# Latent attention block: block 3's scores as two lanes of 64 rows, and Pool's row moves dealt out behind heads

## The chip, the cores and the metric

The kernel runs on one core of one Trainium2 chip. The core has a matrix engine (TensorE, PE in the profile; its weight loads are shown apart as PEld), a vector engine (DVE), a scalar engine (ACT), a general engine (Pool), a queue engine that issues most transfers (SP), and 16 DMA engines. Matmul results go to PSUM, a memory of eight banks of 512 float32 columns on 128 partitions; all other tiles lie in SBUF. The metric is the device time of one execution in microseconds.

## The reference, cut to what matters

One layer: multi-head latent attention over 2048 tokens with a causal mask, a residual and a layer norm, then a linear layer with another residual and norm. 16 heads have 128 content dimensions and 64 rotary dimensions; the rotary part of the key is shared by all heads.

```python
cq = rms_norm(hidden_states @ w_qa.T, q_a_ln_w)                 # 2048 x 384
q = (cq @ w_qb.T).reshape(b, s, H, DQ).transpose(0, 2, 1, 3)    # H = 16, DQ = 128 + 64
q_nope, q_pe = q[..., :DN], q[..., DN:]
q_pe = q_pe * cos + rotate_half(q_pe) * sin
ckv = hidden_states @ w_kva.T                                   # 2048 x (128 + 64)
k_pe = ckv[..., KVLR:]; k_pe = k_pe * cos + rotate_half(k_pe) * sin
ckv_l = rms_norm(ckv[..., :KVLR], kv_a_ln_w)
kv = (ckv_l @ w_kvb.T).reshape(b, s, H, DN + DV).transpose(0, 2, 1, 3)
scores = (q_nope . k_nope + q_pe . k_pe) * scale                # per head, causal
attn = softmax(scores); out = attn . v
x = layernorm(x + out @ w_o.T)
x = layernorm(x + x @ (weight * scale_weight).T + bias)
```

## The kernel before, in words

The key projection is folded into the queries, so that all heads share one key of 128 latent rows. Precision is kept by splitting every operand into a high and a low float16 part: `Kn[:, 0]` and `Kn[:, 1]` are the high and low parts of the latent keys (128 rows, 2048 columns), `qn` the same for the queries. For the rotary part, a tile `pe` holds the high part of a head's 64 rotary query rows in partitions 0 to 63 and the low part in 64 to 127; `Kp[:, 0]` holds the rotary keys' high part in both halves of the partitions, `Kp[:, 1]` their low part. A score chunk is thus five matmuls of 128 rows (`score`, L682): qn high by Kn high, qn high by Kn low, qn low by Kn high, and pe by Kp high and by Kp low. The last of them also multiplies low by low.

The work goes by four query blocks of 512 rows (`b`), in each by eight pairs of heads (`p`), in a pair by four query tiles of 128 rows (`qt`), and for blocks 1 to 3 by the two heads `j` of the pair (`units`, L983). Block 3 comes last and has the longest rows: a query tile sees 1664, 1792, 1920 or 2048 keys for qt 0 to 3. `chunks` (L44) cuts them into four: two of 512, and two of 320, 384, 448 or 512. The first two chunks make the head's first score tile, the last two its second; a tile takes two PSUM banks. Block 3 has three such tiles in rotation ("s", "s", "u" by `state["turn"]`, L728); the other two banks are the tiles "m" of values and projections.

For each head `head_scores` (L714) issues, in this order: the score matmuls of the first tile, its maximum on DVE (L740), the next steps of the head before (`next(prev)`), the score matmuls of the second tile, its maximum, then the bias (L750), two exponentials on ACT with their sums (L756), and the inverse of the sum (L768, L769). `head_probs` is that generator `prev`: ACT writes the high half of the scaled probabilities (L777, two cuts), DVE the low half (L780, two cuts), and SP transposes them into `ring` (L784). In block 3 the first cut of L780 stands between the two maxima for qt 2 and 3 and behind them for qt 0 and 1 (L744). The causal mask lies in the last tile's last 128 columns: as a matmul of `identb` by `maskb` (L697) for j = 0, as an addition on DVE (L701) for j = 1, right behind the tile's matmuls.

Between heads PE has other work, in program order: half of the value products of an earlier query tile (`values`, L822; the lag is two query tiles in block 3), and the projections for the next pair, spread by `at` (L990 to L1005): `project_nope` behind heads 3 and 4 of a pair, `project_pe` behind heads 0 and 1 of every second pair. `project_pe` (L607) makes the rotary rows of four heads at once: PE and DVE make the products (L564, L569), Pool combines them (L631, L632), copies eight groups of 32 high rows into `pe` (L635) and, after ACT has rounded them (L638), writes eight groups of low rows (L640). A group serves two pairs, and it is made while the pair two ahead of its first use runs.

From query tile 1 of block 3's first pair on, the order on PE, SP, DVE and ACT is the order of the code (`manual_schedule`, L1009); Pool's is left to the scheduler. Before that a scheduler orders DVE, ACT and Pool.

Of the kernel before, what the change touches and what calls it, by code (L numbers as in the profile page):

```python
# [19 lines left out]
P = 128  # L20
# [6 lines left out]
QB = 512  # L27
NPAIR = H // 2
# [8 lines left out]
W_O = 32768.0  # L37
X_UP = 1024.0
PROBS = 10240
TINY = 1.0e-30  # L40
NEG = -1.0e30

# [16 lines left out]
def mla_block(ctx: ExitStack, tc: tile.TileContext, a, out):  # L59
    nc = tc.nc  # L60
    ET = mybir.EngineType
# [32 lines left out]
    identb = const.tile([P, P], BF16, name="identb")  # L94
    nc.vector.tensor_copy(identb, ident)
    maskb = const.tile([P, P], BF16, name="maskb")
# [28 lines left out]
    Kn = kv.tile([P, 2, S], F16, name="Kn")  # L125
    Kp = kv.tile([P, 2, S], F16, name="Kp")
# [14 lines left out]
    psum = {}  # L141
# [366 lines left out]
    state = {"queue": nc.sync}  # L508
    later = []
# [74 lines left out]
    def rope_stack(pe, ph, cols, js, eng=nc.vector):  # L584

        for j in js:
            q = slice(32 * j, 32 * j + 32)
            for x in range(2):
                yield eng.tensor_copy(pe[32 * x : 32 * x + 32, j, cols], ph[q, 0, x, cols])
                yield eng.tensor_copy(pe[64 + 32 * x : 96 + 32 * x, j, cols], ph[q, 1, x, cols])  # L590

    stack, soon = [], []

    def run_soon():
        while soon:
            soon.pop(0)()
# [10 lines left out]
    def project_pe(b, g):  # L607

        if ("wpe", b, g) not in state:
            load_wpe(b, g)  # L610
        w = state.pop(("wpe", b, g))
        cq, cs = state["cq"], state["cs"]
        every = slice(0, QB)
        prod = prj.tile([P, 2, 2, QB], F32, tag="prod", name=f"prod{b}_{g}")
        for x in range(2):
            ps = psum["m"].tile([P, QB], F32, tag="m", name=f"ps_pe{b}_{g}_{x}")
            rope_products(w, cq, cs, prod, ps, x, every)
            if x == 0:
                yield
            elif b or g == 3:  # L620
                load_wpe(*((b, g + 1) if g < 3 else (b + 1, 0)))
        ph = prj.tile([P, 2, 2, QB], F16, tag="ph", name=f"ph{b}_{g}")
        pe = blk.tile([P, 8 if (b, g) == (0, 3) else 4, QB], F16, tag="pe", name=f"pe{b}_{g}")
        if b == 0 or (b, g) == (1, 0):
            rope_split(b, prod, ph, every, (nc.gpsimd, nc.gpsimd), nc.vector)
            stack.append(rope_stack(pe, ph, every, range(2 if b else 4)))
            for _ in rope_stack(pe, ph, every, range(2, 4 if b else 2), nc.gpsimd):
                pass
        else:
            rp, tp = prod[:, 0], prod[:, 1]  # L630
            nc.gpsimd.tensor_tensor(rp[:, 0, :], rp[:, 0, :], rp[:, 1, :], ALU.subtract)  # L631
            nc.gpsimd.tensor_tensor(rp[:, 1, :], tp[:, 0, :], tp[:, 1, :], ALU.add)  # L632
            rows = [(j, x, slice(32 * j, 32 * j + 32)) for j in range(4) for x in range(2)]
            for j, x, q in rows:
                nc.gpsimd.tensor_copy(pe[32 * x : 32 * x + 32, j, :], rp[q, x, :])  # L635

            def low_rows():
                nc.scalar.activation(ph[:, 0], rp, AF.Copy)  # L638
                for j, x, q in rows:
                    nc.gpsimd.tensor_tensor(  # L640
                        pe[64 + 32 * x : 96 + 32 * x, j, :], rp[q, x, :], ph[q, 0, x, :], ALU.subtract
                    )

            soon.append(low_rows)
        state["pe", b, g] = pe
        yield
# [56 lines left out]

    def take(n):

        at = state.get("probs_at", 0)
        if at + n > PROBS:
            at = 0  # L710
        state["probs_at"] = at + n
        return probs_mem[:, at : at + n]

    def head_scores(pools, b, p, j, qt, nk, prev):  # L714
        r = er[1][:, p // 2 : p // 2 + 1]
        cks = chunks(nk)
        nt = len(cks)
        neg = small.tile([P, 2], F32, tag="neg", name="neg")
        tiles = []
        for ti, ck in enumerate(cks):  # L720

            if b == 2 and ti == 1:
                ps = psum["t"].tile([P, 1, 512], F32, tag="t", name=f"s{b}_{p}_{qt}_{j}_{ti}", bufs=2)
            else:
                k = "s"
                if b == 3:

                    state["turn"] = (state.get("turn", -1) + 1) % 3  # L728
                    k = "ssu"[state["turn"]]
                ps = psum[k].tile(  # L730
                    [P, 2, 512], F32, tag=k, name=f"s{b}_{p}_{qt}_{j}_{ti}", bufs=3 if b == 1 else 1 if k == "u" else 2
                )
            w = ck[0][1]
            for ci, (c0, w) in enumerate(ck):
                d = nk - P - c0
                score(ps[:, ci, :], c0, w, b, p, j, qt, d if 0 <= d < w else None)
            v = ps[:, : len(ck), :w]
            if ti == nt - 1 == 0:
                next(prev, None)
            nc.vector.tensor_reduce(neg[:, ti : ti + 1], v, axis=AX.XY, op=ALU.max, negate=True)  # L740
            tiles.append((v, ck[0][0], len(ck), w))
            if ti < nt - 1:
                next(prev, None)
                if b < NB - 1 or qt > 1 and (p, qt, j) != (NPAIR - 1, 3, 1):  # L744
                    next(prev, None)
        bias = small.tile([P, 1], F32, tag="bias", name="bias")
        if nt == 1:
            nc.vector.tensor_scalar(bias, neg[:, 0:1], r, None, ALU.mult)
        else:
            nc.vector.tensor_scalar(bias, neg[:, 0:1], neg[:, 1:2], r, ALU.min, ALU.mult)  # L750
        for _ in prev:
            pass
        pr = take(nk)
        sums = small.tile([P, 2], F32, tag="sums", name="sums")
        for ti, (v, c0, n, w) in enumerate(tiles):
            nc.scalar.activation(  # L756
                pr[:, c0 : c0 + n * w].rearrange("p (a c) -> p a c", a=n),
                v,
                AF.Exp,
                bias=bias,  # L760
                scale=r,
                accum_out=sums[:, ti : ti + 1],
            )
        inv = small.tile([P, 1], F32, tag="inv", name="inv")
        if nt == 1:
            nc.vector.tensor_scalar(inv, sums[:, 0:1], 1.0 / P_UP, None, ALU.mult)
        else:
            nc.vector.tensor_scalar(inv, sums[:, 0:1], sums[:, 1:2], 1.0 / P_UP, ALU.add, ALU.mult)  # L768
        nc.vector.reciprocal(inv, inv)  # L769
        return pr, inv  # L770
# [114 lines left out]
    with tc.manual_schedule(engines={ET.PE}):  # L885
        x = [split_x(0, [x_r[0][:, kt : kt + 2] for kt in (0, 2)], nc.gpsimd)]
# [36 lines left out]
        ph = prj.tile([P, 2, 2, QB], F16, tag="ph", name="ph0_0")  # L923
        pe = state["pe", 0, 0] = blk.tile([P, 4, QB], F16, tag="pe", name="pe0_0")
# [58 lines left out]
    def units(pool, ring, b, norms=None):  # L983
        lag = min(ring.shape[1] // (2048 * (b + 1)) - 1, 3) if b else 4

        for p in range(NPAIR):
# [7 lines left out]
            else:  # L994
                at = (3, 4)
# [10 lines left out]
            for qt in range(4):  # L1006
                nk = (4 * b + qt + 1) * P
                if (b, p, qt) == (NB - 1, 0, 1):
                    ctx_f.enter_context(tc.manual_schedule(engines={ET.PE, ET.SP, ET.DVE, ET.Activation}))  # L1009
                if (b, p) == (0, NPAIR - 1) and qt >= 2:  # L1010
                    spare = state["qn", 0, p][:, 2:] if qt == 2 else state["pe", 0, 3][:, 4:]
                    s0 = -4 * nk
# [7 lines left out]
                if nk <= 512:  # L1020
                    pi = pair_scores(pool, b, p, qt, nk)
                    probs.append(pair_probs(pool, b, p, qt, nk, PT, *pi))
                    flush()
                    for step in plan[p][qt]:
                        if step == "F":
                            fill()
                        else:
                            next(side[step == "W"], None)
                    move_rows(6)
                    run_values(lag)  # L1030
                    run_values(lag)
                else:
                    for j in range(2):
                        prepare_output(b, p, 2 * qt + j)
                        prev = probs.pop() if probs else iter(())
                        pi = head_scores(pool, b, p, j, qt, nk, prev)
                        probs.append(head_probs(pool, b, p, j, qt, nk, PT, *pi))
                        if (b, p, qt, j) == (1, 0, 1, 0):
                            half_values()
                            half_values()  # L1040
                        run_soon()
                        if 2 * qt + j in at:
                            fill()
                        if b == 2 and (2 * qt + j) % 4 == 2:
                            next(norms, None)
                        run_values(lag)
# [103 lines left out]
    while len(vals) > 2:  # L1150
# [5 lines left out]
    ring = ctx_m.enter_context(tc.tile_pool(name="rings", bufs=1, reuse_waits="tile")).tile(  # L1156
        [P, 12 * 2048], F16, name="ring"
    )
    probs_mem = ctx_m.enter_context(tc.tile_pool(name="probs", bufs=1, reuse_waits="tile")).tile(
        [P, PROBS], F32, name="probs"  # L1160
    )
# [253 lines left out]
```

## Time and profile before

| | us |
|---|---|
| median of the runs (three: 1507.42, 1507.46, 1510.05) | 1507.46 |
| the profiled execution | 1508.39 |
| its span | 1506.6 |
| PE busy | 1455.3 |
| DVE busy | 1168.2 |
| ACT busy | 937.7 |
| POOL busy | 355.2 |
| block 3's scores, first to last (812.57 to 1262) | 449.4 |

Times in the profile are microseconds from the span's start unless marked ns. A row of the timeline is start, duration, engine, line, operation, output<-input with shapes, how many, and in brackets how long the engine was idle before it and what released it. A row of a window is its bounds and length, then the busy time of PE, PEld, DVE, ACT and POOL with the number of instructions, the granted clock of PE as a share of full speed, the share of the DMA engines and GB/s. Matmuls overlap: a row's duration includes the way through the array, and the step from one start to the next is what a matmul costs in a stream.

### The profile page before, as it was taken

Reading aid. Unit: us, or ns where it says so; the run is one execution under the profiler, and the core shown is the slowest. Engines: PE = TensorE matmul, PEld = TensorE weight load, DVE = VectorE, ACT = ScalarE, POOL = GpSimd, SP = SyncE. Lnnn points to the kernel's source line nnn. Section 1 sums busy time; section 2 is a strip of 40 time slices with the busy share of each in tenths; the row PEclk is TensorE's granted clock in tenths of the full one; section 3 lists DMA queues with packets and bytes.
Section 4 is the critical chain, followed back from the end, with each engine's and each line's share of the span. In section 5 each row is a group of like instructions: output and inputs, shape, how many; then the busy total and the mean of one; then the engine's idle time right before and its main releaser. Section 6 shows DMA issues by size and latency. Waiting matters only on the chain.

```text
span 1506.6 us, 24573 instructions
## 1 busy us (share of the span) xinstructions
PE 1455.3 (97%) x9056; PEld 907.1 (60%) x9056; DVE 1168.2 (78%) x2173; ACT 937.7 (62%) x1695; POOL 355.2 (24%) x412
## 2 busy tenths in 40 slices
PE   8899988999999999999999999999999999999997
PEld 6667754666665566666666666666666665544444
DVE  4787787988888988888888877877877786476654
ACT  6577775666675787778776666666666675432300
POOL 4223313451305405050023500500500000032132
PEclk9899999999999999999999999999999999999999
DMA  5569775878887998989896787787787898655431
GB/s 202 145 162 218 176 183 112 159 146 171 160 186 154 177 189 175 196 179 175 163 199 137 152 163 154 149 163 154 138 159 156 187 217 172 244 155 146 147 92 42
DMA packets 642377, 246.90 MB, mean 164 GB/s; under 512 B 598864, under 2 KB 619600, under 8 KB 641616
## 3 DMA queue, kind: packets, MB, share of 16 engines
q1 hardware_dynamic: 640800, 243.46, 75.1%
q8 instruction: 71, 1.16, 0.3%
q10 hardware_dynamic: 1152, 1.31, 0.3%
q0 software_dynamic: 304, 0.56, 0.1%
q14 instruction: 50, 0.41, 0.1%
HBM read 67.57 MB, written 28.05 MB: 63 GB/s over the span
## 4 chain that ended last, share of the span: by engine, by line
PE 63%; DVE 3%; DMA 1%; issue 1%; ACT 1%; POOL 0%; POOLq 0%; DVEq 0%; ACTq 0%; SPq 0%
PE s L695 27%; PE o L833 17%; PE acc L1134 9%; PE ps_qn L653 4%; PE ff L1283 3%; PE ps_pe L564 2%; PE ps_wo L297 1%; DVE probs L780 1%; DMA ring<-probs 1%; DVE neg L740 1%; ACT probs L756 0%; DMA xt<-xs 0%; DVE bn L1244 0%; ACT probs L777 0%; DVE x L1256 0%
## 5 line engine op out<-in xcount | busy, mean ns | idle before, releaser
L695 PE MATMUL s<-Kn,qn 128*128 128x512 f16 (+5 forms) x1920 | 462.9, 347 | 9.7 <-DVE qn L73 4.9
L756 ACT ACTIVATE probs<-s,bias,er 128x1024 f32<-128x1024 f32 (+3 forms) x320 | 324.1, 1016 | 204.4 <-issue 68.4
L780 DVE SCALAR_TENSOR_TENSOR probs<-probs,inv 128x1024 f16<-128x1024 f32 (+7 forms) x320 | 355.0, 1130 | 28.3 <-ACT probs L777 26.4
L833 PEld LDWEIGHTS <-V 128*128 128x128 f16 x3264 | 319.1, 98 | 87.2 <-issue 15.1
L833 PE MATMUL o<-ring,V 128*128 128x256 f16 x3024 | 361.0, 273 | 2.0 <-DMA ring<-probs 1.3
L740 DVE TENSOR_REDUCE neg<-s 128x1 f32<-128x1024 f32 (+3 forms) x320 | 316.9, 993 | 38.2 <-PE s L695 34.7
L695 PE MATMUL s<-Kp,pe 128*128 128x512 f16 (+5 forms) x1280 | 340.1, 347 | 0.9 <-DVE pe L590 0.9
L777 ACT ACTIVATE probs<-probs,inv 128x1024 f16<-128x1024 f32 (+7 forms) x320 | 294.2, 959 | 72.7 <-DVE inv L769 50.0
L695 PEld LDWEIGHTS <-qn 128*128 128x128 f16 x1920 | 187.6, 98 | 154.3 <-issue 13.7
L695 PEld LDWEIGHTS <-pe 128*128 128x128 f16 x1280 | 124.6, 98 | 107.3 <-DVE pe L590 1.6
L653 PE MATMUL ps_qn<-cq,wq 128*128 128x512 f16 (+1 forms) x594 | 139.2, 382 | 7.6 <-ACT ot L838 3.6
L640 POOL TENSOR_TENSOR pe<-prod,ph 32x512 f16<-32x512 f32 x88 | 123.8, 1407 | 5.7
L1134 PE MATMUL acc<-wvo,oh 128*128 128x512 f16 (+1 forms) x424 | 124.1, 375 | 0.9 <-ACT probs L756 0.9
L631 POOL TENSOR_TENSOR prod<-prod 128x512 f32<-128x512 f32 x11 | 14.0, 1271 | 443.8 <-DVE prod L569 443.8
L653 PEld LDWEIGHTS <-wq 128*128 128x128 f16 x594 | 59.4, 101 | 70.5 <-issue 12.7
L1134 PE MATMUL acc<-wvo,ol 128*128 128x512 f16 (+1 forms) x212 | 79.5, 375 | 0.0
L768 DVE TENSOR_SCALAR inv<-sums 128x1 f32<-128x1 f32 x128 | 26.9, 210 | 66.0 <-ACT probs L756 65.4
L72 ACT ACTIVATE oh<-o,kvo 128x1024 f16<-128x1024 f32 x26 | 29.8, 1146 | 71.0 <-PE acc L1134 58.0
L1134 PEld LDWEIGHTS <-oh 128*128 128x128 f16 x424 | 41.5, 98 | 50.8 <-issue 5.2
L635 POOL CAST pe<-prod 32x512 f16<-32x512 f32 x88 | 66.6, 757 | 14.0 <-PE o L833 10.6
L564 PE MATMUL ps_pe<-cq,wpe 128*128 128x512 f16 (+1 forms) x306 | 68.2, 367 | 1.7 <-DVE wpe L73 0.9
L838 ACT ACTIVATE ot<-o 128x256 f32<-128x256 f32 x128 | 48.3, 378 | 28.7 <-PE o L833 27.6
(214 smaller groups left out, 1553.9 us busy)
## 6 DMA issues: line engine op xcount, KB each, us to landing
ot_d<-ot SPq DMA_DIRECT2D x128, 128.0 KB, 2.6
o<-ot_d SPq DMA_DIRECT2D x32, 512.0 KB, 4.0
wq<-wq_d SPq DMA_DIRECT2D x30, 384.0 KB, 3.8
wpe<-wpe_d SPq DMA_DIRECT2D x15, 384.0 KB, 3.7
nw<-in_wo_dram SPq DMA_DIRECT2D x8, 512.0 KB, 4.2
wo<-in_wo_dram SPq DMA_DIRECT2D x4, 1024.0 KB, 5.6
x<-in_x_dram SPq DMA_DIRECT2D x16, 256.0 KB, 3.5
out_dram<-xb SPq DMA_DIRECT2D x15, 256.0 KB, 2.0
```

Source lines behind the costliest of these rows:

```text
L564: nc.tensor.matmul(ps, w[:, i, lt, x * P : (x + 1) * P], cq[:, tiles(cols), k, lt], start=n == 0, stop=n == 3 * LT - 1)
L635: nc.gpsimd.tensor_copy(pe[32 * x : 32 * x + 32, j, :], rp[q, x, :])
L640: nc.gpsimd.tensor_tensor(pe[64 + 32 * x : 96 + 32 * x, j, :], rp[q, x, :], ph[q, 0, x, :], ALU.subtract)
L653: nc.tensor.matmul(ps, w[:, i, lt, j * P : (j + 1) * P], cq[:, tiles(cols), k, lt], start=n == 0, stop=n == 3 * LT - 1)
L695: nc.tensor.matmul(ps[:, :w], lhs, K[:, i, c0 : c0 + w], start=n == 0, stop=n == 4)
L740: nc.vector.tensor_reduce(neg[:, ti : ti + 1], v, axis=AX.XY, op=ALU.max, negate=True)
L756: nc.scalar.activation(pr[:, c0 : c0 + n * w].rearrange("p (a c) -> p a c", a=n), v, AF.Exp, bias=bias, scale=r, accum_out=sums[:, ti : ti ...
L777: nc.scalar.activation(hl[:, 0, c], pr[:, c], AF.Copy, scale=inv)
L780: nc.vector.scalar_tensor_tensor(hl[:, 1, c], pr[:, c], inv, hl[:, 0, c], ALU.mult, ALU.subtract)
L833: nc.tensor.matmul(ps[:, :256], vt[:, k % 4, i, :], v[:, :, l, k, :], start=n == 0, stop=n == 3 * kts - 1)
L838: nc.scalar.activation(ot, ps[:, :256], AF.Copy)
L1134: nc.tensor.matmul(acc[:, cols], l[:, t, c], state["wvo"][p][:, i, j, cols], start=p == 0 and j == 0 and n == 0, stop=p == NPAIR - 1 and j ...
```

## The change

In block 3 (`b >= ROWS`) a head's scores are made by a new function, `scores_by_rows`. A matmul of 128 rows becomes two of 64: the lower one on partitions 0 to 63, the upper one on 64 to 127, each on a part of the array of its own. The two lanes work at the same time on two key chunks, which lie in two PSUM banks. There are four rounds: (0,1), (2,3), (1,0), (3,2), the first number being the chunk of the lower lane. In a round each lane runs high by Kn high, high by Kn low, low by Kn high, and its half of pe by Kp high. The product of the rotary high rows by Kp low is made once, in the first two rounds; for the upper lane the high rows are needed on partitions 64 to 127, and a new tile `again` holds that copy, written by a DMA on SP, once a pair (`rope_again`). The product of low by low is left out. A chunk so takes nine halves, and a head 36 matmuls and 36 weight loads in 18 steps where it had 20.

Between rounds one and three, and two and four, a lane meets a bank that the other lane has written. An empty Pool instruction (`keepalive_nop`) waits for the earlier round, and the later round waits for it.

Both score tiles of a head are taken before its first matmul, and all its score matmuls are issued before its first maximum. The mask matmul of j = 0 comes last; the mask addition of j = 1 is issued on DVE ahead of both maxima.

Pool's order is the code's too from the same point on. For the rotary groups 1 to 3 of block 3, the eight high-row copies and eight low-row subtractions are no longer issued at once but dealt out behind the following heads, three copies or two subtractions behind each (`by_pool`).

```diff
+ROWS = 3
...
+    by_pool = []
...
-            for j, x, q in rows:
+
+            def high_row(j, x, q):
                 nc.gpsimd.tensor_copy(pe[32 * x : 32 * x + 32, j, :], rp[q, x, :])
+
+            def low_row(j, x, q):
+                nc.gpsimd.tensor_tensor(
+                    pe[64 + 32 * x : 96 + 32 * x, j, :], rp[q, x, :], ph[q, 0, x, :], ALU.subtract
+                )
+
+            later = b >= ROWS and g > 0
+            for r in rows:
+                if later:
+                    by_pool.append((3, lambda r=r: high_row(*r)))
+                else:
+                    high_row(*r)
+            if later:
+                by_pool.extend((2, lambda r=r: low_row(*r)) for r in rows)
 
             def low_rows():
                 nc.scalar.activation(ph[:, 0], rp, AF.Copy)
-                for j, x, q in rows:
-                    nc.gpsimd.tensor_tensor(
-                        pe[64 + 32 * x : 96 + 32 * x, j, :], rp[q, x, :], ph[q, 0, x, :], ALU.subtract
-                    )
+                if not later:
+                    for r in rows:
+                        low_row(*r)
...
+    def rope_again(b, p):
+
+        again = state["again", b, p] = psum["again"].tile([P, 2, QB], F16, tag="again", name=f"again{b}_{p}")
+        nc.sync.dma_start(again[64:], state["pe", b, p // 2][:64, 2 * (p % 2) : 2 * (p % 2) + 2])
+
+    def scores_by_rows(parts, b, p, j, qt, masked):
+
+        qs = slice(qt * P, (qt + 1) * P)
+        qn = state["qn", b, p]
+        high, low = qn[:, 0, j, qs], qn[:, 1, j, qs]
+        rope, again = state["pe", b, p // 2][:, 2 * (p % 2) + j, qs], state["again", b, p][:, j, qs]
+        upper = [slice(0, 64), slice(64, P)]
+        left = {n: 9 for n in range(4)}
+        left[3] += masked is not None
+        last = set()
+
+        def add(n, lhs, rhs):
+            ps, c0, w = parts[n]
+            begin = n not in last
+            left[n] -= 1
+            return nc.tensor.matmul(ps[:, :w], lhs, rhs, start=begin, stop=left[n] == 0)
+
+        for lanes in ((0, 1), (2, 3), (1, 0), (3, 2)):
+            first = lanes[0] < lanes[1]
+            ops = [(high, Kn, 0), (high, Kn, 1), (low, Kn, 0), (rope, Kp, 0)]
+            if first:
+                ops.append((None, Kp, 1))
+            for at, (lhs, K, i) in enumerate(ops):
+                for lane, n in enumerate(lanes):
+                    c0, w = parts[n][1:]
+                    rows = upper[lane]
+                    w_ = lhs if lhs is not None else (rope, again)[lane]
+                    ins = add(n, w_[rows], K[rows, i, c0 : c0 + w])
+                    last.add(n)
+            if first:
+                nc.gpsimd.keepalive_nop([nc.gpsimd.lower_ap(parts[n][0][:, : parts[n][2]]) for n in lanes])
+        if masked is not None:
+            ps = parts[3][0]
+            nc.tensor.matmul(ps[:, masked : masked + P], identb, maskb, start=False, stop=True)
...
+        if b >= ROWS:
+            made, parts = [], []
+            for ti, ck in enumerate(cks):
+                state["turn"] = (state.get("turn", -1) + 1) % 3
+                k = "ssu"[state["turn"]]
+                ps = psum[k].tile([P, 2, 512], F32, tag=k, name=f"s{b}_{p}_{qt}_{j}_{ti}", bufs=1 if k == "u" else 2)
+                made.append(ps)
+                parts += [(ps[:, ci], c0, w) for ci, (c0, w) in enumerate(ck)]
+            d = nk - P - parts[3][1]
+            scores_by_rows(parts, b, p, j, qt, d if j == 0 else None)
+            if j:
+                dg = parts[3][0][:, d : d + P]
+                nc.vector.tensor_tensor(dg, dg, maskb, ALU.add)
         for ti, ck in enumerate(cks):
 
-            if b == 2 and ti == 1:
+            if b >= ROWS:
+                ps = made[ti]
+            elif b == 2 and ti == 1:
...
             for ci, (c0, w) in enumerate(ck):
+                if b >= ROWS:
+                    continue
...
-                    ctx_f.enter_context(tc.manual_schedule(engines={ET.PE, ET.SP, ET.DVE, ET.Activation}))
+                    ctx_f.enter_context(tc.manual_schedule(engines={ET.PE, ET.SP, ET.DVE, ET.Activation, ET.Pool}))
...
                         run_soon()
+                        for _ in range(by_pool[0][0] if by_pool else 0):
+                            if by_pool:
+                                by_pool.pop(0)[1]()
+                        if b >= ROWS and (qt, j) == (0, 1) and p + 1 < NPAIR:
+                            rope_again(b, p + 1)
+                        if b == ROWS - 1 and p == NPAIR - 1 and (qt, j) == (3, 0):
+                            rope_again(ROWS, 0)
...
+    psum["again"] = ctx_m.enter_context(tc.tile_pool(name="again", bufs=2, reuse_waits="tile"))
```

More of the change, by code (lines that the diff above doesn't have):

```diff
@@ L39 @@
 PROBS = 10240
+ROWS = 3
+SYNC = mybir.DependencyInfo(mybir.DependencyClass.Sync, mybir.DependencyReason.DATA)
 TINY = 1.0e-30
```

## The prediction

> **What bounds the kernel now.** I read the page first (busy shares and the chain that ended last), then block 3's stretch in the windows view and its waits, then the timeline of a few heads there. The page:
>
> ```profile
> PE 1455.3 (97%) x9056; PEld 907.1 (60%) x9056; DVE 1168.2 (78%) x2173; ACT 937.7 (62%) x1695; POOL 355.2 (24%) x412
> ...
> PE 63%; DVE 3%; DMA 1%; issue 1%; ACT 1%; POOL 0%; POOLq 0%; DVEq 0%; ACTq 0%; SPq 0%
> PE s L695 27%; PE o L833 17%; PE acc L1134 9%; PE ps_qn L653 4%; PE ff L1283 3%; PE ps_pe L564 2%; PE ps_wo L297 1%; DVE probs L780 1%; DMA ring<-probs 1%; DVE neg L740 1%; ACT probs L756 0%; DMA xt<-xs 0%; DVE bn L1244 0%; ACT probs L777 0%; DVE x L1256 0%
> ```
>
> TensorE carries the chain, and the score matmuls (L695) are its largest part. A busy PE need not be a PE at its peak, so I looked at block 3 alone, from its first score matmul to its last (the windows view), and at what PE waited for there:
>
> ```profile
> 812.57:1262.00 449.43, 447.86 (x2891) 281.79 (x2889) 355.57 (x513) 301.80 (x444) 61.64 (x56) 1.00 0.82 161
> ...
> PE s L695 <- ACT probs L756: 0.5, 1, 0.5
> ```
>
> PE is busy 447.9 of 449.4 us at full clock, DVE 355.6 (79%), ACT 301.8. Matmuls of one line start at even steps: 216 ns for 512 columns, 189 for 448, 162 for 384, 136 for 320, 109 for 256. PE is bound by streaming. But the one wait named is the one that matters for this change, a score matmul waiting for an exponential (ACT L756). The timeline of block 3 from the last head of one pair to the first head of the next:
>
> ```profile
> 867.99 1.21 DVE L740 TENSOR_REDUCE neg<-s 128x1 f32<-128x1024 f32 x1
> ...
> 869.25 2.46 PE L833 MATMUL o<-ring,V 128*128 128x256 f16 x21
> 869.35 1.28 DVE L780 SCALAR_TENSOR_TENSOR probs<-probs,inv 128x1024 f16<-128x1024 f32 x1 [0.15 <-ACT probs L777]
> 870.55 0.29 DVE L701 TENSOR_TENSOR s<-s,maskb 128x128 f32<-128x128 f32 x1
> ...
> 870.88 1.22 DVE L740 TENSOR_REDUCE neg<-s 128x1 f32<-128x1024 f32 x1
> 871.54 0.81 PE L695 MATMUL s<-Kn,qn 128*128 128x512 f16 x3
> ...
> 872.14 0.27 DVE L750 TENSOR_SCALAR bias<-neg,er 128x1 f32<-128x1 f32 x1
> ...
> 872.50 1.21 ACT L756 ACTIVATE probs<-s,bias,er 128x1024 f32<-128x1024 f32 x1 [2.14 <-PE o L833]
> ...
> 873.27 0.59 PE L695 MATMUL s<-Kp,pe 128*128 128x512 f16 x2
> ...
> 873.85 0.57 PE L695 MATMUL s<-Kn,qn 128*128 128x320 f16 x3
> ...
> 875.34 1.94 DVE L740 TENSOR_REDUCE neg<-s 128x1 f32<-128x1024 f32 x2
> ```
>
> Block 3 has three score buffers and each head takes two, so a head's second tile (chunks 2 and 3) is the buffer of the previous head's first tile and waits for that tile's exponential. Here the second tile starts at 873.85, 1.35 us after the exponential (872.50) started, and 0.15 us after PE was ready (873.27 plus two steps). The buffer is free just in time: no slack is left.
>
> **The change, part by part.** Each sum is against the profiled execution, 1508.39 us with a span of 1506.6; the median of the runs shown is 0.9 lower.
>
> *Fewer slots: a gain.* A head's four chunks take 5 full matmuls each, 20 slots. Afterwards each chunk takes 9 halves, two lanes at once: 18 slots. One 512 slot goes, and one of 320, 384, 448 or 512 by qt: 0.352, 0.378, 0.405, 0.432 us. Over 16 heads of each: 25.1 us, all of it on PE, which is the bound. No row shows 64-row matmuls. Ends: a pair takes one slot (the gain stands), or two (36 slots a head, 16 more, at a mean slot of 196 ns and 64 heads: +201 us). I take one slot, since the lanes have rows and output chunks apart, and keep the other end as a rival.
>
> The Trainium skill (TensorE: Matmul & The Clock Gate, section "Measured speedup vs the span model") says that four row tiles together gave 3.07 times, not 4; an estimate from that page, two lanes at the same efficiency, would be 23.5 slots instead of 18, about 69 us more, and no run here shows it.
>
> *The order of the rounds: a loss, and the largest term.* The rounds are (0,1), (2,3), (1,0), (3,2) with 5, 5, 4, 4 slots. Two things follow. The second tile is wanted after 5 slots (1.08 us) instead of 10 (2.16). And the first tile is complete after 14 slots, not 10, so its reduction moves towards the end of the scores. On top, for head j=1 the mask add on the second tile is now issued ahead of both reductions; DVE works in order, so behind that add, which waits for the last score matmul, stand the reduction of tile 0, the low half of the previous head's probabilities (L780; between the reductions for qt 2 and 3) and the reduction of tile 1. The exponential waits for all of these, and the next head's second round waits for it.
>
> Steps from the rows above and two more:
>
> ```profile
> 1004.92 0.59 PE L695 MATMUL s<-Kp,pe 128*128 128x512 f16 x2
> ...
> 1005.35 0.65 PE L695 MATMUL s<-Kn,qn 128*128 128x384 f16 x3
> ...
> 1005.55 1.23 DVE L740 TENSOR_REDUCE neg<-s 128x1 f32<-128x1024 f32 x1 [0.70 <-PE s L695]
> ```
>
> The last slot ends at 1005.35 and the reduction starts 0.20 later. Mask add to an independent next instruction: 0.21 (0.29 less the 0.08 by which DVE rows overlap). Reduction of tile 0: 1.12 (875.34, two with 1.94, the second 0.82). L780: 1.20 (869.35 to 870.55). Reduction of tile 1 to bias 1.26, bias to exponential 0.36, exponential to PE 1.35. From the end of a head's scores:
> - qt 3, j=1: 0.20+0.21+1.12+1.20+1.26+0.36+1.35 = 5.70. PE has 21 value matmuls (2.29) and the first round (1.08), 3.37. It waits 2.3, at 7 pair boundaries: 16.3 us.
> - qt 2, j=1: a tile of 896 columns and L780 of 960 make it 5.50; less 3.37 is 2.1, 8 times: 17.0.
> - qt 3, j=0: no DVE mask, and tile 0 was complete 4 slots earlier: -0.66+1.12+1.20+1.26+0.36+1.35 = 4.63, less 3.37 and the mask matmul's 0.06: 1.2, 8 times: 9.6.
> - qt 0, j=1: no L780 between, second tile 640: 4.10 against 24 value matmuls and the round, 3.70: 0.4, 8 times: 3.2.
> - The other heads: the two before projections (nine L653 matmuls, 1.94 more) and j=0 of qt 0 and 1 (about 3.4 against 3.37) wait nothing.
>
> Together 46.1 us of new PE waiting. It replaces the waits that are there now, 0.15 at seven boundaries and about 0.7 near 1250: 1.8.
>
> *Changing the array's shape.* Each head enters and leaves the 64-row form: 128 changes. No row shows one. Below: nothing, as a change of line is free now (the values start at 869.25, two steps of 0.216 after the last two score matmuls began at 868.82). Above: the tail of a matmul past its slot (379-216 = 163 ns) and a weight load (98 ns), 0.26 us. I take the tail, the row nearest to emptying the array. At the 23 long waits both changes lie inside the wait and cost nothing, and at the 8 short ones about half do; 74 are left: 12 us (ends 0 and 19).
>
> The Trainium skill (TensorEngine Tiling (Array Packing), section "Key Properties") says that changing the tiling mode drains TensorE. It speaks against the change and gives no figure; no trace here shows it yet. By the rule this term is not nothing; by the rows' lower end it is.
>
> *Weight loads.* 36 instead of 20 a head, two per slot, 98 ns in the rows (L695 PEld). If two cannot overlap, a slot is at least 196 ns: 9 slots of 136, 162 and 189 ns grow by 60, 34 and 7 ns in 16 heads each, 14.5 us. I take nothing: around a mask matmul two loads start 0.06 us apart (PEld rows at 874.79 and 874.85). Ends 0 and 14.5.
>
> *The empty Pool instructions.* Two a head. Round three waits for one that waits for round one; round two (0.68 to 1.08 us) covers the way, 0.20 to Pool and about as much back. Round three covers the second. Behind a waiting one stand Pool's row moves, which nobody needs for a pair. What stands ahead of it can block it: L631 and L632 wait for DVE (L569), three times in block 3. In the trace L632 had started at 831.26, and PE would want round three of that head (830.42 plus 2.16) at 832.58. Nothing; ends 0 and 3 times 1.3, 4 us.
>
> *Pool's moves.* The same 16 instructions a group (0.79 and 1.44 us), now 2 or 3 behind a head, 2.4 to 2.9 us of a head's 6. Cover: the group is first read a pair later. Without it: one group's 18 us, seen three times as a PE wait.
>
> *The copies of the high rows.* Eight DMAs of 128 KB on SP. One like it (ot_d, 128 KB) takes SP 0.6 us and lands in 2.6. SP has a transpose of about 4 to 5.6 us per head, and values run two query tiles, four heads, behind the probabilities; that lag hides it. If it did not: 8 times 0.6, 5 us. PE reads the copy only in the next pair.
>
> Sum: -25.1 - 1.8 + 46.1 + 12 = +31 us; 1539.6 for the profiled execution, 1539 as a median.
>
> **The rivals.**
> - *Full gain* (ends faster): the second round does not wait. Gain 25.1 less 128 changes at 0 to 0.163 us (21): 1482 to 1503. For it: PE is the bound and DVE has 21% idle. Against it: the 0.15 us wait already there. It decides from the point where new waiting and shape changes together stay under 27 us, below 0.86 us at each of the 31 boundaries.
> - *Lanes one after another*: +201; the second round is then wanted 1.08 us later, the three long waits shrink to about 1.2, 1.0 and 0.1 us (17 us); with the shape changes about 1736. Against it: rows and banks are separate.
> - *Waits plus dear shape changes and loads*: 46.1 - 26.9 + 19 + 14.5 = +53, about 1560.
> - *Balanced*: waits of half the size, changes free: 23 - 27 = -4 to 0, about 1505 to 1508.
>
> **How the numbers follow.** Forecast 0.78, 1539; without the two unknown prices it is 1527, and with waits a fifth smaller 1518. Dear changes 0.09, to 1560. Lanes in turn 0.05. Full gain 0.05. Balanced 0.03, of which half within 0.2%. The range 1518 to 1560 leaves out less than 2 in 10. Faster 0.06, same 0.02, slower 0.92; 0.2% (3 us) is about what a measurement of this kernel tells from no change, its three runs lying 2.6 us apart.
>
> **What would show it.** In block 3 PE idle ahead of the second tile's first matmul, released by the exponential (ACT L756 now), some 46 us in all, 2 us at qt 3 and at the pair's start; DVE's mask add waiting for PE at the head of each j=1 group; the slot at 216 ns per pair of 512 columns; gaps of 0 to 0.26 us at a change of shape; next to no PE wait for Pool. The forecast is wrong if pairs take clearly more than one slot, or if the waits before the second round are small.

## The result, and the profile after

The changed kernel takes 1542.96 us (median of five runs, 1536.69 to 1545.22) against 1507.46 before; the ratio over all runs is 1.0221, 95% interval 1.0208 to 1.0233. Its profiled execution took 1536.69 us, with a span of 1534.9; it is the fastest of the five, 28.3 us above the profiled execution of before.

The page of the changed kernel, busy time by engine and the chain that ended last. Its line numbers are its own: L743 is a 64-row score matmul, L712 a score matmul of blocks 0 to 2, L907 a value matmul, L830 the exponential, L814 the maximum, L854 the low half, L758 the empty Pool instruction.

```profile
PE 1449.2 (94%) x10080; PEld 890.9 (58%) x10080; DVE 1161.6 (76%) x2173; ACT 937.3 (61%) x1695; POOL 344.4 (22%) x412
...
PE 58%; DVE 4%; issue 4%; ACT 2%; DMA 1%; POOL 0%; SPq 0%; POOLq 0%; DVEq 0%; ACTq 0%
PE o L907 15%; PE s L743 13%; PE s L712 11%; PE acc L1215 9%; PE ps_qn L670 3%; PE ff L1365 2%; PE ps_pe L566 2%; DVE probs L854 1%; DVE neg L814 1%; ACT probs L830 1%; PE ps_wo L299 1%; DMA ring<-probs 1%; DMA xt<-xs 0%; ACT probs L851 0%; DVE bn L1326 0%
```

PE fell from 97% of the span to 94%, and its share of the chain from 63% to 58%. Block 3, from its first score matmul to the end of its last, in the windows view (bounds, length, then busy time of PE, PEld, DVE, ACT and POOL with counts, PE clock, DMA share, GB/s):

```profile
811.00:1289.40 478.40, 440.27 (x3906) 263.72 (x3906) 347.61 (x514) 301.14 (x444) 49.66 (x54) 1.00 0.79 154
```

The window of before was 449.4 us, of which PE was busy in all but 1.6; now it is 478.4, of which PE is idle for 38, at full clock. (The window of before ends at 1262, 1.3 us behind the last score matmul. From the first score matmul's start to the last one's, block 3 took 447.9 us before and takes 477.7 now.) What PE waited for there (engine, tile and line, releaser, us in all, times, longest):

```profile
PE s L743 <- ACT probs L830: 34.5, 23, 1.9
PE s L743 <- DMA again<-pe: 2.0, 1, 2.0
PE s L743 <- POOLq L758: 1.3, 2, 0.6
```

Almost all of it is a score matmul waiting for an exponential. The timeline at the start of a pair (start, duration, engine, line, operation):

```profile
1050.91 0.40 PE L743 MATMUL s<-Kp,pe 64*128 64x512 f16 x2
...
1051.24 2.47 PE L907 MATMUL o<-ring,V 128*128 128x256 f16 x21
1051.35 0.30 DVE L789 TENSOR_TENSOR s<-s,maskb 128x128 f32<-128x128 f32 x1 [1.44 <-PE s L743]
1051.56 1.21 DVE L814 TENSOR_REDUCE neg<-s 128x1 f32<-128x1024 f32 x1
1052.68 1.28 DVE L854 SCALAR_TENSOR_TENSOR probs<-probs,inv 128x1024 f16<-128x1024 f32 x1
...
1053.64 0.33 PEld L743 LDWEIGHTS <-qn 64*128 64x128 f16 x6 [0.21 <-issue]
1053.64 0.82 PE L743 MATMUL s<-Kn,qn 64*128 64x512 f16 x6
1053.88 1.22 DVE L814 TENSOR_REDUCE neg<-s 128x1 f32<-128x1024 f32 x1
...
1055.13 0.27 DVE L824 TENSOR_SCALAR bias<-neg,er 128x1 f32<-128x1 f32 x1
...
1055.49 1.20 ACT L830 ACTIVATE probs<-s,bias,er 128x1024 f32<-128x1024 f32 x1 [3.30 <-PE s L743]
...
1056.84 0.58 PE L743 MATMUL s<-Kn,qn 64*128 64x320 f16 x6 [1.94 <-ACT probs L830]
```

The last slot of a head of qt 3, j=1 starts at 1050.91 and ends one step of 0.216 later, at 1051.13. Then DVE runs the mask add, the first maximum, the first part of the low half of the head before, the second maximum and the bias, in that order and without a gap, and ACT the exponential. At 1056.84, 5.71 us after the scores ended, the next head's second round may start. Its first round had begun at 1053.64 and was done 1.08 us later, so PE stood still for 2.1 us.

Between PE's starts in this trace, the two matmuls of a pair stand 2 to 6 ns apart in two thirds of the pairs and 16 to 20 ns in the others, and slots 216, 189, 162 or 136 ns apart: two lanes cost one slot. The way into the 64-row form shows as 96 ns between the step of the last 128-row matmul and the first pair, the way out as 92 to 113 ns.

The 28.3 us between the two profiled executions, from the steps between PE's starts:

| | us |
|---|---|
| two slots fewer a head, 64 heads | -25.1 |
| waits before a second round, 39.3 now against 1.8 before | +37.5 |
| 128 changes of the array's form, 6.1 in and 6.7 out | +12.8 |
| PE waits for the first copy of the high rows | +2.0 |
| PE waits for the empty Pool instruction, twice | +1.6 |
| sum | +28.8 |

The table leaves out that the first step behind each change is some 10 ns longer (1.3 us in 128). With it the sum is 30.1, against 29.8 by which block 3's scores grew. PE came to block 3 1.5 us sooner than before (811.02 against 812.57); in the traces of the experiments that moment lies anywhere from 811.0 to 814.0.

### The profile page after: what moved, and what is told of

Same layout as the page of the kernel before. It is cut to its first block, busy times and chain, and to the rows that moved or that the text cites. A ratio compares the mean times of both kernels' runs of the same rounds, so it can differ in the third digit from the quotient of the medians.

```text
span 1534.9 us, 26766 instructions
## 1 busy us (share of the span) xinstructions
PE 1449.2 (94%) x10080; PEld 890.9 (58%) x10080; DVE 1161.6 (76%) x2173; ACT 937.3 (61%) x1695; POOL 344.4 (22%) x412
## 4 chain that ended last, share of the span: by engine, by line
PE 58%; DVE 4%; issue 4%; ACT 2%; DMA 1%; POOL 0%; SPq 0%; POOLq 0%; DVEq 0%; ACTq 0%
PE o L907 15%; PE s L743 13%; PE s L712 11%; PE acc L1215 9%; PE ps_qn L670 3%; PE ff L1365 2%; PE ps_pe L566 2%; DVE probs L854 1%; DVE neg L814 1%; ACT probs L830 1%; PE ps_wo L299 1%; DMA ring<-probs 1%; DMA xt<-xs 0%; ACT probs L851 0%; DVE bn L1326 0%
## 5 line engine op out<-in xcount | busy, mean ns | idle before, releaser
L830 ACT ACTIVATE probs<-s,bias,er 128x1024 f32<-128x1024 f32 (+3 forms) x320 | 324.1, 1016 | 238.8 <-DVE bias L824 74.3
L854 DVE SCALAR_TENSOR_TENSOR probs<-probs,inv 128x1024 f16<-128x1024 f32 (+7 forms) x320 | 349.5, 1113 | 27.6 <-ACT probs L851 26.4
L907 PEld LDWEIGHTS <-V 128*128 128x128 f16 x3264 | 316.8, 98 | 86.6 <-issue 21.8
L907 PE MATMUL o<-ring,V 128*128 128x256 f16 x3024 | 361.2, 273 | 1.1 <-DMA ring<-probs 0.5
L814 DVE TENSOR_REDUCE neg<-s 128x1 f32<-128x1024 f32 (+3 forms) x320 | 314.9, 992 | 34.9 <-PE s L743 23.3
L712 PE MATMUL s<-Kn,qn 128*128 128x512 f16 (+5 forms) x1152 | 268.9, 340 | 8.6 <-DVE qn L75 4.4
L743 PE MATMUL s<-Kn,qn 64*128 64x512 f16 (+3 forms) x1536 | 194.7, 357 | 35.9 <-ACT probs L830 34.5
L712 PE MATMUL s<-Kp,pe 128*128 128x512 f16 (+5 forms) x768 | 198.1, 340 | 0.9 <-DVE pe L592 0.9
L712 PEld LDWEIGHTS <-qn 128*128 128x128 f16 x1152 | 112.4, 98 | 84.9 <-issue 10.0
L743 PEld LDWEIGHTS <-qn 64*128 64x128 f16 x1536 | 73.8, 94 | 116.3 <-issue 58.3
L642 POOL TENSOR_TENSOR pe<-prod,ph 32x512 f16<-32x512 f32 x88 | 116.9, 1329 | 71.8 <-PE s L743 66.7
L743 PE MATMUL s<-Kp,pe 64*128 64x512 f16 (+3 forms) x640 | 118.1, 356 | 0.0
L712 PEld LDWEIGHTS <-pe 128*128 128x128 f16 x768 | 74.5, 98 | 59.6 <-DVE pe L592 1.6
L634 POOL TENSOR_TENSOR prod<-prod 128x512 f32<-128x512 f32 x11 | 14.0, 1269 | 405.7 <-DVE prod L571 262.0
L74 ACT ACTIVATE oh<-o,kvo 128x1024 f16<-128x1024 f32 x26 | 29.8, 1145 | 69.9 <-PE acc L1215 58.0
L639 POOL CAST pe<-prod 32x512 f16<-32x512 f32 x88 | 62.2, 707 | 43.2 <-PE s L743 29.7
```

The source lines that it names most:

```text
L642: nc.gpsimd.tensor_tensor(pe[64 + 32 * x : 96 + 32 * x, j, :], rp[q, x, :], ph[q, 0, x, :], ALU.subtract)
L712: nc.tensor.matmul(ps[:, :w], lhs, K[:, i, c0 : c0 + w], start=n == 0, stop=n == 4)
L743: return nc.tensor.matmul(ps[:, :w], lhs, rhs, start=begin, stop=left[n] == 0)
L830: nc.scalar.activation(pr[:, c0 : c0 + n * w].rearrange("p (a c) -> p a c", a=n), v, AF.Exp, bias=bias, scale=r, accum_out=sums[:, ti : ti ...
L854: nc.vector.scalar_tensor_tensor(hl[:, 1, c], pr[:, c], inv, hl[:, 0, c], ALU.mult, ALU.subtract)
L907: nc.tensor.matmul(ps[:, :256], vt[:, k % 4, i, :], v[:, :, l, k, :], start=n == 0, stop=n == 3 * kts - 1)
```

## The experiments

Two theories were held against each other. W: DVE's chain behind a head's scores is too long for a second tile that is wanted after five slots, and PE waits. T: the 64-row form itself costs the time. In each experiment the printed edit is against the changed kernel, unless it says otherwise, and times are compared with those of the kernel before in the same round (medians of 1508.4 to 1508.6).

### The mask add moved behind the first maximum

```diff
-            if j:
-                dg = parts[3][0][:, d : d + P]
-                nc.vector.tensor_tensor(dg, dg, maskb, ALU.add)
         for ti, ck in enumerate(cks):
...
+            if b >= ROWS and ti == nt - 1 and j:
+                dg = parts[3][0][:, d : d + P]
+                nc.vector.tensor_tensor(dg, dg, maskb, ALU.add)
             nc.vector.tensor_reduce(neg[:, ti : ti + 1], v, axis=AX.XY, op=ALU.max, negate=True)
```

> The changed kernel, with one line moved: DVE's mask add for j=1 stands directly ahead of the second tile's maximum instead of ahead of both. Theory W (PE waits before the second round because DVE's chain behind a head's scores is long): behind j=1 heads of qt 2 and 3 the maximum of tile 0 starts about 0.85 us sooner, the wait shrinks from 2.1 to 1.4 us at the pair's start and from 1.9 to 1.3 at qt 3; 7 x 0.74 + 8 x 0.62 + 8 x 0.2 = some 12 us less than the changed kernel, a profiled span near 1523 (1534.9 there). Theory T (the 64-row form itself costs the time: shape changes, loads, a lower clock): no change, within 3 us.

Measured: 1529.1 us, 1.0137 of before (1.0123 to 1.0151); span 1526.0, 8.9 us under the changed kernel's where 12 were expected. PE's waits in block 3 now:

```profile
PE s L743 <- ACT probs L830: 27.1, 23, 1.5
PE s L743 <- DMA again<-pe: 2.4, 1, 2.4
...
```

The order of one 0.3 us instruction on DVE is worth 9 us of the span (by the medians 14); under T nothing would have changed. It is less than expected because, by the steps between PE's starts, the waits at a pair's start fell by 0.4 or 0.7 us and those at qt 3, j=0 by 0.3 or 0.6, from pair to pair in turn, and the third kind not at all.

### The low half moved behind both maxima

```diff
                 next(prev, None)
-                if b < NB - 1 or qt > 1 and (p, qt, j) != (NPAIR - 1, 3, 1):
+                if b < NB - 1:
                     next(prev, None)
```

> The changed kernel, with the first cut of the previous head's low half (L854) behind both maxima for all qt of block 3, not between them for qt 2 and 3. Theory W: 1.2 us leave the chain behind every head of qt 2 and 3; waits go from 2.1 to 0.9 (pair's start), 1.9 to 0.8 (qt 3, j=0), 0.9 to 0 (qt 3, j=1); 7 x 1.2 + 8 x 1.1 + 8 x 0.9 = some 24 us less, a span near 1511. Theory T: no change. A rival within W, that the low half then comes too late for SP's transposes and the values: PE waits for the ring appear in the place of the waits removed, over 10 us of them.

Measured: 1512.36 us, 1.0029 (1.0017 to 1.0041); span 1509.8, 25.1 under the changed kernel's. Waits:

```profile
PE s L743 <- ACT probs L830: 9.8, 15, 0.8
...
PE o L907 <- DMA ring<-probs: 0.9, 2, 0.7
```

This is W's number. The rival within W, a ring that comes too late, is 0.9 us and not 10.

### Both moves

Both edits above, and nothing else.

> Both moves together: mask add late and low half late. Theory W: the waits before the second round all but go (0.2 us at the pair's start and at qt 3), some 36 us less than the changed kernel, a span near 1499, with the 25 us of fewer slots left over against 13 us of shape changes and 4 us of other waits: 6 to 8 us faster than before. Theory T: no change from the changed kernel.

Measured: 1500.86 us, 0.9951 of before (0.9937 to 0.9964); span 1499.4. The kernel is faster than before, by 0.5%. Block 3 in the windows view, and its waits, all of them:

```profile
811.00:1256.00 445.00, 439.09 (x3915) 262.14 (x3913) 350.11 (x515) 302.28 (x445) 49.83 (x55) 1.00 0.86 165
...
PE o L907 <- DMA ring<-probs: 2.8, 2, 2.2
PE s L743 <- DMA again<-pe: 2.1, 1, 2.1
PE s L743 <- POOLq L758: 0.5, 2, 0.2
PE s L743 <- ACT probs L830: 0.3, 1, 0.3
```

The timeline at a pair's start in this kernel, to be held against the one above:

```profile
1036.42 1.20 ACT L830 ACTIVATE probs<-s,bias,er 128x1024 f32<-128x1024 f32 x1 [1.58 <-issue]
...
1036.49 0.82 PE L743 MATMUL s<-Kn,qn 64*128 64x512 f16 x6
...
1037.77 0.58 PE L743 MATMUL s<-Kn,qn 64*128 64x320 f16 x6
```

The exponential of the old first tile starts before the next head's scores do; the second round follows the first with a gap of 0.2 us. The 64-row form, its 128 changes and its fences (the empty Pool instructions) are all still there, so T is out: they cost less than the two slots gain. PE waits for the exponential 0.3 us in all, where it waited 34.5.

### Both moves, and the first copy issued earlier

```diff
-                        if b == ROWS - 1 and p == NPAIR - 1 and (qt, j) == (3, 0):
+                        if b == ROWS - 1 and p == NPAIR - 1 and (qt, j) == (2, 1):
                             rope_again(ROWS, 0)
```

> As the one with both moves, and the copy of the high rows for block 3's first pair is issued on SP two heads earlier (head 5 of block 2's last pair instead of head 6). Theory W: the 2.0 us in which PE waits for that copy at the start of block 3 goes, the rest stays: a span near 1497, 9 us faster than before. Theory T: as the changed kernel.

Both moves stand in this run too.

Measured: 1502.98 us, 0.9963 (0.9951 to 0.9975): a miss. PE no longer waits for the copy, but the first head's second round waits 0.7 us for an exponential instead, and the span is 1502.6, 3.2 us longer than with both moves alone. In this trace the granted clock (the last but two of the columns) falls twice behind stretches in which PE was idle, for 2.0 of 6.8 us and for 3.1 of 7.0:

```profile
1214.50:1221.30 6.80, 4.81 (x40) 2.38 (x37) 5.28 (x9) 4.83 (x9) 0.00 (x0) 0.95 1.17 236
1221.30:1224.70 3.40, 3.40 (x21) 2.51 (x20) 2.79 (x5) 3.40 (x6) 0.00 (x0) 0.59 1.01 282
1432.00:1439.00 7.00, 3.87 (x19) 1.61 (x18) 4.34 (x5) 0.93 (x3) 3.95 (x4) 1.00 0.97 205
1439.00:1442.40 3.40, 3.40 (x10) 1.22 (x9) 1.15 (x3) 0.63 (x1) 0.00 (x0) 0.51 0.62 141
```

Two windows of 3.4 us at about half clock are some 3 us of PE, the distance from both moves alone. The trace with both moves has the same two idle stretches and no fall behind either. Here is the first of them there, to be held against the first two rows above:

```profile
1213.80:1220.60 6.80, 4.62 (x40) 1.99 (x41) 5.54 (x9) 4.83 (x9) 0.00 (x0) 1.00 1.17 242
1220.60:1224.00 3.40, 3.40 (x32) 2.58 (x34) 2.79 (x5) 3.40 (x6) 0.00 (x0) 1.00 0.96 294
```

The second stretch lies in the last layer, where the kernel before (at 1442.5) and the changed kernel (at 1471.1) have such a window too. So the earlier copy saves a wait of 2.1 us and brings 1.6 back at the exponential (1.9 against 0.3), and the clock makes most of the rest. What makes the clock fall behind one such stretch and not behind another is open, and so is whether it explains the other five executions, which left no trace.

### The kernel before with the order on DVE alone

The old 128-row matmuls in the old order, but all of a head's score matmuls issued before its first maximum, so that DVE meets the mask add first. The edit is against the kernel before.

```diff
+        if b == 3:
+            made = []
+            for ti, ck in enumerate(cks):
+                state["turn"] = (state.get("turn", -1) + 1) % 3
+                k = "ssu"[state["turn"]]
+                ps = psum[k].tile([P, 2, 512], F32, tag=k, name=f"s{b}_{p}_{qt}_{j}_{ti}", bufs=1 if k == "u" else 2)
+                made.append(ps)
+                for ci, (c0, w) in enumerate(ck):
+                    d = nk - P - c0
+                    score(ps[:, ci, :], c0, w, b, p, j, qt, d if 0 <= d < w else None)
         for ti, ck in enumerate(cks):
 
-            if b == 2 and ti == 1:
+            if b == 3:
+                ps = made[ti]
+            elif b == 2 and ti == 1:
...
             for ci, (c0, w) in enumerate(ck):
+                if b == 3:
+                    continue
```

> The kernel before, full 128-row matmuls in the old order on PE, with only the order on DVE of the change: in block 3 all score matmuls of a head are issued before its first maximum, so the mask add of j=1 stands ahead of both maxima. No Pool fence, no 64-row form, no dealing. Theory W: behind j=1 of qt 3 the chain from the end of the scores is 5.70 us against 2.29 of values and 2.16 of the first tile's ten matmuls, 1.25 us of wait at 7 pair starts; behind j=1 of qt 2 5.50 against 4.45, 1.05 us 8 times; together 17 us slower than before, a span near 1523. Theory T (the 64-row form is the cost): as before, 1507.

Measured: 1522.33 us, 1.0092 (1.0077 to 1.0107); span 1522.2. The waits, and DVE's order behind a head:

```profile
PE s L695 <- ACT probs L766: 14.7, 15, 1.1
...
```

```profile
871.58 0.30 DVE L701 TENSOR_TENSOR s<-s,maskb 128x128 f32<-128x128 f32 x1 [0.78 <-PE s L695]
871.78 1.22 DVE L750 TENSOR_REDUCE neg<-s 128x1 f32<-128x1024 f32 x1
872.91 1.27 DVE L790 SCALAR_TENSOR_TENSOR probs<-probs,inv 128x1024 f16<-128x1024 f32 x1
874.11 1.22 DVE L750 TENSOR_REDUCE neg<-s 128x1 f32<-128x1024 f32 x1
```

There are fifteen waits: sixteen heads have j=1 and qt 2 or 3, and one of them is the block's last, with no head behind it. The order alone, with nothing of the 64-row form, costs some 14 us.

### The kernel before with Pool's dealing alone

The edit is against the kernel before. Pool's order is the code's from the same point as in the changed kernel.

```diff
...
+            later = b >= 3 and g > 0
+            for r in rows:
+                if later:
+                    by_pool.append((3, lambda r=r: high_row(*r)))
+                else:
+                    high_row(*r)
+            if later:
+                by_pool.extend((2, lambda r=r: low_row(*r)) for r in rows)
...
+                        for _ in range(by_pool[0][0] if by_pool else 0):
+                            if by_pool:
+                                by_pool.pop(0)[1]()
```

> The kernel before with only Pool's part of the change: the row moves of block 3's groups 1 to 3 dealt out behind heads, Pool in the code's order from the same point. Every theory: nothing, within 1 us, since each group is first read a pair later and no one else waits for Pool in that stretch.

Measured: 1508.41 us, 1.0002 (0.9992 to 1.0011). No difference, as expected.

### Both moves, Pool's row moves not dealt out

```diff
-            later = b >= ROWS and g > 0
+            later = False
```

Both moves stand in this run too.

> The kernel with both moves (mask add and low half late), and Pool's row moves issued all at once as before, still with the 64-row rounds and the empty Pool instruction. Theory Q1 (the empty instruction runs on Pool's sequencer and passes row moves that are already handed over): only as many moves fit ahead as the engine's queue takes; eight copies and eight subtractions are 18 us of work in three groups, so PE waits some 10 to 12 us in each of them, about 35 us more than with dealing, near 1536. Theory Q2 (it passes them all): no change from the kernel with both moves, 1501.

Measured: 1531.79 us, 1.016 (1.0142 to 1.0179); span 1528.9, 29.5 over that with both moves. The waits, one of the six in the timeline, and two windows, in the columns of above:

```profile
PE s L743 <- POOLq L758: 19.2, 6, 4.6
...
```

```profile
1075.25 1.26 POOL L635 TENSOR_TENSOR prod<-prod 128x512 f32<-128x512 f32 x1
1076.45 2.58 POOL L639 CAST pe<-prod 32x512 f16<-32x512 f32 x4
...
1078.47 1.10 PE L743 MATMUL s<-Kn,qn 64*128 64x512 f16 x6 [3.44 <-POOLq L758]
```

```profile
846.80:853.60 6.80, 5.12 (x21) 1.89 (x21) 3.07 (x5) 0.22 (x1) 6.40 (x7) 0.50 0.36 77
...
1078.90:1082.30 3.40, 3.40 (x20) 1.76 (x17) 1.99 (x2) 0.00 (x0) 2.56 (x5) 0.50 0.01 2
```

Eight copies stand ahead of the empty instruction. PE goes on at 1078.47, when the fourth copy has just begun (1076.45 plus three of 0.65), not when the eighth is done. In all six waits the empty instruction runs 0.02 to 0.04 us before the fourth of eight moves begins, so it passes five moves that have not begun. That fits Q1's mechanism, by which it waits until the moves ahead are handed over and not until they are done; Q2 is out.

Q1's size is another matter. It expected PE to wait 10 to 12 us in each of three groups, and PE waits 19.2 in all. Most of the rest of the 29.5 is clock: in five windows of block 3, 20.4 us together, the granted clock is half, each time in or shortly behind one of these waits, and with both moves there is no such window in block 3. PE was busy for 18 us of them, so an estimate from these rows is 9 us lost. The dealing that is worth nothing in the kernel before is worth 30 us here, about two thirds of it as waits for Pool.

### Both moves, the rounds in another order

```diff
-        for lanes in ((0, 1), (2, 3), (1, 0), (3, 2)):
+        for lanes in ((0, 1), (1, 0), (2, 3), (3, 2)):
```

> The kernel with both moves, its rounds in the order (0,1), (1,0), (2,3), (3,2): the empty Pool instruction stands between rounds that follow each other at once, so nothing covers it. It prices the fence: the tail of the last matmul (about 0.16 us past its slot), the way to Pool and the way back, twice a head. At 0.4 to 0.6 us each, 128 times, 50 to 75 us less the waits for the exponential (under 6 us), which go as the second tile is wanted four slots later: near 1550 to 1570. If the fence were nearly free: 1500.

Both moves stand in this run too.

Measured: 1534.43 us (two runs), 1.0172 (1.0152 to 1.0192). The fence, that is the empty Pool instruction between two rounds, is now uncovered. It shows in PE's steps as a gap of 0.27 us ahead of the second round and 0.28 us ahead of the fourth, in every head:

```profile
1018.49 0.38 PE L743 MATMUL s<-Kp,again 64*128 64x512 f16 x1
1018.98 0.82 PE L743 MATMUL s<-Kn,qn 64*128 64x512 f16 x6
```

From 1018.49 to 1018.98 are 0.49 us, one slot of 0.216 and 0.27 more. Together 0.56 a head, 36 us for 64 heads; the span of 1532.9 is 33.5 over that with both moves. The expectation had about twice that, 0.4 to 0.6 us each. If the matmul's tail past its slot is the 0.16 of the rows (0.38 less 0.216; ends of matmuls are modelled in the profile), the way to Pool and back is only some 0.11.

## Why the prediction was right

The forecast of 1539 us lies 4 us under the median and 2 us over the profiled execution, and its likeliest case is the one that happened: PE waits for the exponential before the second round. That the number is so near is partly luck, since the changes of shape were put too high and two waits at nothing, and the two errors nearly cancel. By its steps:

- *Fewer slots*: right. A pair of lanes takes one slot, at all widths; -25.1 us stands.
- *The order of the rounds, and the mask add ahead of both maxima*: right in mechanism and close in size. At the heads named, PE waits 2.1 us (7 times), 1.9 and 0.9 to 1.25; the prediction had 2.3, 2.1 and 1.2 with two changes of form inside, 2.1, 1.9 and 1.0 if these are taken out at the 0.1 us each that the rows show. Its 46.1 us in all become 39.9 so, and 39.3 were measured. The chain of 5.70 us from the end of the scores measured 5.71. The run with the old matmuls shows the order on DVE at work by itself, and the three runs with moves that the waits go when that order goes. The order of the rounds was not run by itself: what it adds to the 14.7 us of waits with the old matmuls, up to the 34.5 here, is shown by the chain's sum only.
- *Changing the array's shape*: the term that was mis-sized. It took a matmul's tail of 163 ns; the rows show 96 in and 92 to 113 out, so that the 74 changes outside waits cost about 7 us and not 12. The Trainium skill (TensorEngine Tiling (Array Packing), section "Key Properties") says that a mode change drains TensorE; the trace agrees that a change is not free, with 0.1 us each.
- *Weight loads*: nothing, as taken; slots of 320 columns keep their 136 ns with two loads each.
- *The copies of the high rows*: wrong for the first. It is issued one head ahead of its use at the end of block 2, not a pair ahead as the others are, and PE waited 2.0 us. The prediction put all eight at nothing, with a reason that holds only for the later ones.
- *The empty Pool instructions*: the place was right, the sum not. It took nothing, with ends of 0 and 4 us, and PE waited twice, 0.8 us each: L635 waits for L634 and holds Pool's sequencer, and the empty instruction behind it. In the changed kernel's timeline PE goes 0.03 us after L635:

```profile
951.50 1.27 POOL L634 TENSOR_TENSOR prod<-prod 128x512 f32<-128x512 f32 x1 [71.86 <-PE s L743]
...
952.85 1.27 POOL L635 TENSOR_TENSOR prod<-prod 128x512 f32<-128x512 f32 x1
952.88 0.82 PE L743 MATMUL s<-Kn,qn 64*128 64x512 f16 x6 [0.65 <-POOLq L758]
```

  The trace of before had L632 (L635 here) start 1.3 us ahead of PE's need, and the new order moved that meeting. By the steps the two waits are 0.8 us each with the low half moved too, and 0.4 with the mask add moved, so DVE's order has a part in this as well; the rest was not looked into.
- *Pool's moves*: costed at nothing, and worth nothing by themselves. But the cover was named for their readers only; the run without dealing shows that, with the 64-row rounds, they must be dealt out for the fence's sake.

Of the rivals, the one with lanes in turn is out by the slots, the full gain and the balanced case by the waits, and the dear changes by 0.1 us a change and slots that did not grow. The Trainium skill (TensorE: Matmul & The Clock Gate, section "Measured speedup vs the span model") has a span of one matmul plus some 4 ns for each further tile; the 2 to 6 ns of most pairs here agree and the 16 to 20 ns of the others do not. The prediction's estimate of 69 us from its ratio for four tiles is not borne out, since slots of two lanes keep 216 to 136 ns.

What stays open: the other four executions of the changed kernel are 2 to 8.5 us over the profiled one. Their mean granted clocks were 0.987 to 0.990 against its 0.993, which would fit windows of half clock like those of the fourth experiment and of the one without dealing; they left no trace, so it is not shown. So the 6 us between the profiled execution and the median are not explained.

## What to carry to other kernels

A saving on the engine that bounds a kernel arrives only if what feeds it keeps up at the new moments: ask not only how long the work now takes, but when each buffer is first wanted and when each result is complete. An in-order engine's program is part of the critical path: here two moves on DVE, of instructions that cost the same wherever they stand, turned 2.2% slower into 0.5% faster than before. And a fence that passes through a third engine is cheap as long as other work covers the way and nothing on that engine's sequencer waits ahead of it.

## What the runs showed of the hardware

- Two 64-row matmuls on separate halves of the array start 2 to 20 ns apart and share one slot (216 ns for 512 columns, 136 for 320); a change between the 64-row and the 128-row form costs about 0.1 us each way (96 ns in, 92 to 113 out).
- A fence from PE through Pool back to PE costs 0.27 to 0.28 us past the end of the slot if nothing covers it. It passes five row moves that Pool has not yet begun (six times in the run without dealing), but not a Pool instruction that waits for another's end (0.8 us, twice).
- In the trace of the fourth experiment the granted clock fell to 0.59 and 0.51 for windows of 3.4 us, behind stretches of 7 us in which PE had been idle for 2 and 3 us; in that of the third it stayed at 1.00 behind stretches of the same kind. In the run without dealing five windows of block 3 were at 0.50, in or behind waits of 2.5 to 4.6 us.
